# Input lines of the later parts turned by VectorE in square blocks, and the images loaded in another order of partitions

## The chip, the core and the metric

The kernel runs on one core of a Trainium2 chip. The metric is the device time of one execution in microseconds (us). Most of the work is fp32 matmuls on TensorE (PE); VectorE (DVE), ScalarE (ACT) and GpSimd (POOL) prepare operands and take results away, and SyncE (SP), POOL and ACT issue DMAs.

## What is computed

The input `x` holds 1024 images of 16 x 16 pixels with 16 channels, fp32. Four layers follow, each of them residual on a group-normalised input:

```
x = x + tt_matvec(gn(x), core0, core1, core2)   # layer 0, a tensor-train matrix
x = x + nca(gn(x), weights of L1)               # layer 1
x = x + conv3x3(gn(x), filters, bias)           # layer 2
x = x + nca(gn(x), weights of L3)               # layer 3
```

`gn` is a group norm with 8 groups of 2 channels over an image. The change is in how `x` gets into the kernel for layer 0, before and during that layer's first phase.

## The kernel before, in words

**Layout.** The batch is cut into two chunks of 512 images (`NB` = 512). In memory an image is one row of 4096 values, and a load puts one image on each partition. The matmuls want the transpose: a line `[128, 512]`, whose 128 partitions are 8 columns x 16 channels of one image row `h` and whose 512 elements are the images. A chunk has 32 lines, `(h, wh)` with `h` from 0 to 15 and `wh` 0 or 1 (left or right half of the row).

**Parts.** Layer 0 works on four parts of the lines. Part 0 is `wh = 0` with `h % 8 < 4`: 8 lines a chunk, kept on chip in the tile that `part_tile(0)` gives. All 32 lines are also written to the scratch tensors `xr[n]` in DRAM, from where the later parts and the residual of layer 0 are read back (`load_part`, line 937, from 75% of phase 1 on; `residual`, line 1063, in phases 2 and 3).

**`input_steps` (line 812)** gives the steps for a chunk:

- `load` (line 820): 8 DMAs of 1024 KB, each with 128 images by 8 image rows into one of 8 slots of `XN[1]`. Chunk 0 is loaded by SP, chunk 1 by POOL. A slot of chunk 1 overwrites the one of chunk 0, so a load waits until all readers of the slot are done.
- `stats` (line 827): 8 `bn_stats` on DVE for each slot.
- `turn(h, wh)` (line 836): four 128x128 transposes on PE (line 840) into one PSUM bank, and one copy by ACT into the on-chip part (line 843) or a `lines` tile (line 851). Two lines share one `lines` tile of tag `t4`, of which there are three (`gn = dict(t4=3, ...)`, line 1514), and leave by one POOL DMA of 512 KB (line 853); the on-chip lines leave four at a time by a POOL DMA of 1024 KB (line 845).
- `small`, `newton`, `widen`, `spread` (lines 857 to 890): mean and scale of each image and group, transposed to lines on PE and kept in `mr`.

`normed` (line 903) and `combined` (line 915) then normalise and add up part 0 on DVE.

**Order of the work.** Every engine works off its instructions in the order in which the program issues them. At the start (line 1541) the steps of chunk 0 up to `normed` and `combined` are issued at once (`now`), with 14 of the 32 turns of chunk 0. Then `run` (line 1479) issues phase 0 of layer 0: 64 main steps, four for each of 16 units (u0 to u15; a unit is one output tile pair). A main step is two `T.matmul` calls (four PE records, line 1098) of `pieces` (line 1082). In its first step a unit also builds the weights of the next one (`build`, line 1009: matmuls `pw` at line 1021, ACT copies at line 1026); in its third it asks SP for `gq` data two units ahead (`gload`); in its fourth DVE makes the mixed weight of the next unit (`mix`, line 1031, record L1039), and the next unit's first matmul reads that mixed weight. Between main steps `run` puts background steps, each with a cost: a step becomes due at the share of the main steps that equals the share of the costs ahead of it. In phase 0 the background is, in this order: what is left of chunk 0's turns (`late`) with the loads of chunk 1 among them, eight steps `later` that make the second half of the `g` weights (each pair uses a tile of tag `t4` that ACT fills, line 565), stats and turns of chunk 1 (`woven_in`), the small steps, and `normed` and `combined` for chunk 1. Phase 1 needs these last ones.

Of the kernel before, what the change touches and what calls it, by code (L numbers as in the profile page):

```python
# [19 lines left out]
P = 128  # L20
NB = 512
# [82 lines left out]
def conv_preact_kernel(ctx: ExitStack, tc: tile.TileContext, a: dict, out: bass.AP):  # L104
    nc = tc.nc
    V, A, G, T = nc.vector, nc.scalar, nc.gpsimd, nc.tensor
# [16 lines left out]
    xr = [dram.tile([2, S, P, NB], F32, tag=f"xr{n}", name=f"xr{n}") for n in range(NCH)]  # L123
# [12 lines left out]
    def work(shape, tag, name, dt=F32):  # L136
        p, sizes = pool["sb"]
        return p.tile(shape, dt, tag=tag, name=name, bufs=sizes[tag])
# [23 lines left out]
    ident = const.tile([P, P], F32, tag="ident", name="ident")  # L162
# [649 lines left out]
    def input_steps(n, tag, lag, queue):  # L812

        st = {}
        slots = XN[1].rearrange("p n b -> p (n b)").rearrange("p (s f) -> p s f", s=8)
        X, E = part_tile(0)

        def load(half, bg):  # L820
            b0 = n * NB + bg * P
            queue.dma_start(
                slots[:, 4 * half + bg],
                a["x"][b0 : b0 + P, 8 * half : 8 * half + 8].rearrange("b h w c -> b (h w c)"),
            )

        def stats(half, bg):
            if half == 0 and bg == 0:
                st["b"] = work([P, NB], "s", "bn")[:, 0:384].rearrange(
                    "p (g k f e) -> p g k f e", g=4, k=8, f=2  # L830
                )
            x = slots[:, 4 * half + bg].rearrange("p (q g i) -> p q g i", g=8, i=2)
            for g in range(8):
                V.bn_stats(st["b"][:, bg, g, half], x[:, :, g])

        def turn(h, wh):
            pt = bank([P, 4, P], tag[0], "ptin")
            for bg in range(4):
                x = slots[:, 4 * (h // 8) + bg].rearrange("p (h w f) -> p h w f", h=8, w=2)
                T.transpose(pt[:, bg], x[:, h % 8, wh], ident)  # L840
            pt = pt.rearrange("p g b -> p (g b)")
            if wh == 0 and h % 8 < 4:
                A.copy(X[:, h // 8, h % 4, 1], pt)
                if h % 4 == 3:
                    G.dma_start(
                        xr[n][0, h - 3 : h + 1].rearrange("h p b -> p h b"), X[:, h // 8, :, 1]
                    )
                return
            if h % 2 == 0:
                st["l"] = work([P, 2, NB], "t4", "lines")  # L850
            A.copy(st["l"][:, h % 2], pt)
            if h % 2 == 1:
                G.dma_start(
                    xr[n][wh, h - 1 : h + 1].rearrange("h p b -> p h b"), st["l"]
                )

        def small():
            t = work([P, NB], "n", "small")
            st["mv"] = t[:, 0:64].rearrange("p (g k e) -> p g k e", g=4, k=8)
            st["ve"], st["t"], st["r"] = (  # L860
                t[:, 64 + 32 * j : 96 + 32 * j].rearrange("p (g k) -> p g k", g=4) for j in range(3)
            )
            for bg in range(4):
                for g in range(8):
                    V.bn_aggr(st["mv"][:, bg, g], st["b"][:, bg, g])
            V.tensor_scalar(st["ve"], st["mv"][:, :, :, 1], GN_EPS, None, ALU.add)
            A.activation(st["t"], st["ve"], AF.Sqrt)

        def newton():
            ve, t, r = st["ve"], st["t"], st["r"]  # L870
            V.reciprocal(r, t)
            V.tensor_tensor(t, r, r, ALU.mult)
            V.tensor_tensor(t, t, ve, ALU.mult)
            V.tensor_scalar(t, t, -0.5, 1.5, ALU.mult, ALU.add)
            V.tensor_tensor(r, r, t, ALU.mult)

        def widen(k):
            st["e", k] = e = work([P, NB], "s", "wide").rearrange("p (g f) -> p g f", g=4)
            src = st["mv"][:, :, :, 0] if k == 0 else st["r"]
            for bg in range(4):  # L880
                V.tensor_copy(
                    e[:, bg].rearrange("p (w g i) -> p w g i", w=8, i=2),
                    src[:, bg].unsqueeze(1).unsqueeze(3).broadcast_to([P, 8, 8, 2]),
                )

        def spread(k):
            pt = bank([P, 4, P], tag[0], "ptmr")
            for bg in range(4):
                T.transpose(pt[:, bg], st["e", k][:, bg], ident)
            A.copy(mr[:, k, n], pt.rearrange("p g b -> p (g b)"))  # L890

        loads = [lambda half=half, bg=bg: load(half, bg) for half in range(2) for bg in range(4)]
        stat = [[(2.6, lambda half=half, bg=bg: stats(half, bg)) for bg in range(4)] for half in range(2)]

        lines = [
            [(1, lambda h=h, wh=wh: turn(h, wh)) for wh in range(2) for h in range(8 * half, 8 * half + 8)]
            for half in range(2)
        ]
        tail = [(3, small), 2, (1, newton), (1, lambda: widen(0)), (1, lambda: widen(1)), 1]
        tail += [(0, lambda: spread(0)), lag, (0, lambda: spread(1)), 2]  # L900
        return loads, stat, lines, tail

    def normed(p, n, src=None):

        X, E = part_tile(p)

        def op(b, t, k):
            x = X[:, b, t : t + 2, n]
            y = x if k or src is None else X[:, b, t : t + 2, src]
            m = mr[:, k, n].unsqueeze(1).broadcast_to([P, 2, NB])  # L910
            V.tensor_tensor(x, y, m, ALU.mult if k else ALU.subtract)  # L911

        return [(1.2, lambda b=b, t=t, k=k: op(b, t, k)) for b in range(2) for t in (0, 2) for k in range(2)]
# [605 lines left out]
    def now(steps):  # L1519
        for step in steps:  # L1520
            step = step[1] if isinstance(step, tuple) else step
            if callable(step):
                step()
# [8 lines left out]
    with ExitStack() as es:  # L1532
        stage(es, dict(gn, w=2, r=2, gq=2, R=1), dict(o=3, w=4, m=1))
        setup, later = train_setup(XN[0].rearrange("p n b -> p (n b)")[:, 8192:14336])
# [3 lines left out]

        A.activation(work([P, NB], "n", "warm")[:, 0:1], ident[:, 0:1], AF.Sqrt)
        now(setup[:1])  # L1540
        now(stat[0] + stat[1] + lines[0][:4] + setup[1:] + tail[:1] + lines[1][:4] + tail[1:] + lines[0][4:10])
        start, phases = layer_train()
        start()
        now(normed(0, 0, 1) + combined(0, True))
        tag[0] = "mw"
        late = lines[0][10:] + lines[1][4:]
        loads, stat, lines, tail = input_steps(1, tag, 2, G)
        woven_in = [x for j in range(2) for i in range(4) for x in stat[j][i : i + 1] + lines[j][4 * i : 4 * i + 4]]
        run(
            steps_of(phases[0]), 130, (),  # L1550
            (late[:6] + loads[0:4] + late[6:] + loads[4:] + later + woven_in + tail + normed(0, 1) + combined(0, False), 0.0, 1.0),
        )
        run(
            steps_of(phases[1]), 350, (),
# [82 lines left out]
```

## Time and profile before

| what | value |
|---|---|
| three runs, lowest, median, highest | 3052.58, 3054.53, 3059.36 us |
| the profiled execution's own time | 3054.15 us |
| its span | 3052.4 us (1.75 us lie around it) |
| busy PE, DVE, ACT, POOL | 2982.6, 1757.4, 1100.0, 674.8 us |
| PE first matmul of phase 0 | 50.13 us |
| PE in 50 to 218 us | phase 0 |

Times are us from the span's start unless said otherwise. A row of groups has, after the first bar, the busy us and the mean ns of one instruction, and after the second the idle time of its engine ahead of it and what ended that. In a timeline each row begins with its start and its length in us. Rows of DMA issues have the count, the KB of each and the median us to landing; rows of DMA queues have packets, MB and the share of 16 engines' time.

Where phase 0 ends can be read from two things. DVE's record L1039 comes once for each unit of phase 0; the four together at 216.19 us are for the first unit of phase 1, and are issued in the last unit of phase 0. And PE's `pw` of the second unit of phase 1 begins at 220.34 us, four PE records of about 0.43 us after phase 1 began, so that phase 0 ends at 218.6 us.

### The profile page before, as it was taken

To read this page: it belongs to the slowest core of one execution; us is meant where nothing else is said; L and a number is where in the kernel's file an instruction comes from. 1 tells how busy PE (TensorE), PEld (TensorE's weight loads), DVE (VectorE), ACT (ScalarE), POOL (GpSimd) and SP (SyncE) were. 2 spreads that over 40 slices of the span, in tenths; PEclk is the share of its full clock that TensorE was granted. 3 is DMA by queue.
4 is the path that set the end of the run, shared out by engine and by line. 5 is a ranking of instruction groups with operands and counts; after the bars stand their busy time and mean duration, and the time that the engine had idled before them with its cause. 6 is when DMAs were issued, how large, how long until landed. Compare 5 with 4: busy or idle time off the path is not lost.

```text
span 3052.4 us, 36639 instructions
## 1 busy us (share of the span) xinstructions
PE 2982.6 (98%) x13746; PEld 1252.2 (41%) x13746; DVE 1757.4 (58%) x2338; ACT 1100.0 (36%) x1798; POOL 674.8 (22%) x732
## 2 busy tenths in 40 slices
PE   7999999999999999999999999999999999999996
PEld 5544334444444444444444433333333333333332
DVE  5254336555554555544555768756977766856432
ACT  4431341100000000000111156666667656666563
POOL 1114671200000000000000015434542223442331
PEclk8999999999999999999999999999999999999998
DMA  7642664533333433332222235436337866343555
GB/s 260 257 146 88 137 140 156 179 107 116 109 110 126 151 109 109 109 102 88 88 88 94 71 123 172 132 123 202 123 125 177 193 101 204 123 129 112 149 163 197
DMA packets 251809, 418.67 MB, mean 137 GB/s; under 512 B 35044, under 2 KB 105320, under 8 KB 248560
## 3 DMA queue, kind: packets, MB, share of 16 engines
q1 hardware_dynamic: 225376, 362.45, 35.9%
q0 software_dynamic: 25440, 53.58, 8.5%
q8 instruction: 109, 1.79, 0.2%
q14 instruction: 68, 0.56, 0.1%
q10 hardware_dynamic: 816, 0.30, 0.0%
HBM read 238.79 MB, written 165.60 MB: 132 GB/s over the span
## 4 chain that ended last, share of the span: by engine, by line
issue 47%; PE 43%; POOL 5%; DMA 1%; DVE 1%; ACT 0%; SPq 0%; POOLq 0%; DVEq 0%
PE ph L1466 17%; PE po L1098 13%; PE po L1317 6%; PE po L1193 2%; POOL u L1368 2%; POOL res L1369 2%; PE pw L1021 1%; PE L_conv_pe L392 1%; PE ptin L840 1%; POOL xf L1242 1%; PE ptx L1378 1%; DMA gq<-g_dram 0%; PE pr L739 0%; PE pvar L727 0%; PE pmean L723 0%
## 5 line engine op out<-in xcount | busy, mean ns | idle before, releaser
L1098 PE MATMUL po<-xn,w 128*128 128x512 f32 x3584 | 1577.4, 597 | 4.6 <-DVE xn L911 4.6
L1098 PEld LDWEIGHTS po<-xn,w 128*128 128x128 f32 x3584 | 672.3, 191 | 841.5 <-issue 818.3
L1469 ACT ACTIVATE hid<-ph,pack 128x512 f32<-128x512 f32 x1024 | 652.5, 686 | 380.5 <-PE ph L1466 271.0
L1134 DVE TENSOR_TENSOR r<-r,po 128x512 f32<-128x512 f32 x576 | 378.1, 684 | 577.0 <-PE po L1098 525.9
L1368 POOL TENSOR_TENSOR u<-u,mask 128x512 f32<-128x512 f32 x124 | 195.8, 1579 | 1817.4 <-DMA nx<-xn 1239.7
L1026 ACT COPY w<-pw 128x512 f32<-128x512 f32 (+1 forms) x320 | 150.6, 557 | 1214.4 <-issue 1014.5
L1466 PE MATMUL ph<-xn,wq 32*128 32x512 f32 x3664 | 565.7, 610 | 0.0
L1466 PEld LDWEIGHTS ph<-xn,wq 32*128 32x128 f32 x3664 | 232.8, 184 | 270.2 <-issue 238.2
L1466 PE MATMUL ph<-xn,pack 32*128 32x512 f32 x1288 | 297.5, 623 | 1.2 <-DVE mask L1362 0.9
L1317 PE MATMUL po<-hid,pack 128*32 128x512 f32 x2048 | 282.5, 606 | 2.7 <-ACT hid L1469 2.7
L1039 DVE TENSOR_TENSOR w<-w 128x512 f32<-128x512 f32 x320 | 210.5, 685 | 99.8 <-ACT w L1026 99.8
L640 DVE TENSOR_TENSOR xn<-xn,m 128x1024 f32<-128x1024 f32 x160 | 225.5, 1458 | 47.1 <-ACT m L655 47.0
L1329 DVE SCALAR_TENSOR_TENSOR u<-po,pack,xn 128x512 f32<-128x512 f32 x128 | 95.9, 749 | 204.7 <-PE po L1317 200.3
L1369 POOL TENSOR_TENSOR res<-res,u 128x512 f32<-128x512 f32 x124 | 207.5, 1673 | 9.7
L1193 PE MATMUL po<-xn,convw 128*128 128x512 f32 x368 | 166.8, 606 | 5.1 <-ACT conv L1241 5.1
L1466 PEld LDWEIGHTS ph<-xn,pack 32*128 32x128 f32 x1288 | 115.8, 185 | 98.4 <-issue 62.7
L1134 DVE TENSOR_TENSOR xn<-xn,po 128x512 f32<-128x512 f32 x96 | 64.4, 685 | 125.9 <-PE po L1098 125.8
L1317 PEld LDWEIGHTS po<-hid,pack 128*32 128x32 f32 x2048 | 43.1, 109 | 197.4 <-issue 137.7
L607 DVE TENSOR_TENSOR sq<-sq 128x1024 f32<-128x1024 f32 x78 | 106.9, 1370 | 13.1 <-ACT sq L625 10.8
L1193 PEld LDWEIGHTS po<-xn,convw 128*128 128x128 f32 x368 | 69.2, 193 | 102.1 <-issue 92.0
L404 POOL DMA_DIRECT2D L_conv_wy<-xn x160 | 88.8, 563 | 28.5 <-ACT xn L398 17.6
L1021 PE MATMUL pw<-R,gq 32*128 32x256 f32 (+1 forms) x1280 | 88.9, 383 | 2.3 <-DMA gq<-g_dram 2.3
(165 smaller groups left out, 1775.2 us busy)
## 6 DMA issues: line engine op xcount, KB each, us to landing
xf<-r SPq DMA_DIRECT2D x112, 512.0 KB, 3.9
xn<-xf SPq DMA_DIRECT2D x96, 512.0 KB, 5.0
r<-xf SPq DMA_DIRECT2D x80, 512.0 KB, 4.4
wq<-L_conv_wy SPq DMA_DIRECT2D x192, 192.0 KB, 2.7
res<-xf SPq DMA_DIRECT2D x128, 256.0 KB, 3.0
xf<-res SPq DMA_DIRECT2D x96, 256.0 KB, 2.0
res<-xr SPq DMA_DIRECT2D x256, 64.0 KB, 2.8
xf<-conv POOLq DMA_DIRECT2D x64, 256.0 KB, 6.0
```

The lines of the kernel that those rows point to most:

```text
L640: V.tensor_tensor(part, part, m().unsqueeze(1).broadcast_to([P, 2, NB]), op)
L1021: T.matmul(pw[r][:, v], st["g", u][rows, v], st["R"][rows, p % 2, 64 * k0 : 256], start=True, stop=True,)
L1026: A.copy(w[:, k0:4, :, 32 * r : 32 * r + 32].rearrange("p k t (v o) -> p v (k t) o", v=2), pw[r],)
L1039: V.tensor_tensor(w[:, k], w[:, x], w[:, y], ALU.add if sign > 0 else ALU.subtract)
L1098: T.matmul(po, st["w", u][:, matrix, t], x, start=t == 0, stop=t == 3)
L1134: V.tensor_tensor(r[at], r[at], po, ALU.add if sign > 0 else ALU.subtract)
L1193: T.matmul(st["po", h][wh], conv["fw"][:, y], X[:, 16 * wh + h + y - 1], start=y == max(0, 1 - h), stop=y == min(2, S - h),)
L1317: T.matmul(po[32 * j : 32 * j + 32], nca["w1"][:, v], hid[j], start=v == 0, stop=v == 1)
L1368: by.tensor_tensor(u, u, st["m"][:, w2], ALU.mult)
L1369: by.tensor_tensor(r, r, u, ALU.add)
L1466: T.matmul(ph, w, x, start=k == 0, stop=k == len(tiles) - 1)
L1469: A.activation(h, ph, AF.Relu, bias=nca["bt"][:, r : r + 1])
```

## The change

Only eight lines a chunk are still turned on PE: the lines of part 0 that stay on chip. The other 24 are turned by DVE in 32x32 blocks, written into a `t4` tile and sent to `xr` by POOL. A block transpose moves values only inside a group of 32 partitions, so the images are loaded in another order: partition `32g + j` of slot `bg` holds image `128g + 32bg + j` of the chunk. With that, a block row of 32 partitions gives 128 successive images of a line. The lines turned on PE and the means and scales come out in the order of partitions, and ACT's copy puts them into the order of images (`ordered`, `in_order`).

In numbers, for each chunk:

- loads: 32 DMAs of 256 KB in place of 8 of 1024 KB
- turns on PE: 8 in place of 32
- `blocks(h)`, new: 16 steps. For `h % 8 < 4` only the right half (4 transposes of 128x128 elements, 4 DMAs), else both halves (4 transposes of 128x256 elements, 8 DMAs); each takes one whole `t4` tile. A DMA carries 64 KB: 32 partitions, 4 columns, 128 images.
- stores by POOL: 98 in place of 14

In the start, six turns of chunk 0 disappear, and the order in phase 0 is put together again: 16 `blocks` steps of chunk 0 at a cost of 2.2 each with the loads of chunk 1 among them, then `later`, then stats, 8 turns and 16 `blocks` of chunk 1.

```diff
         def load(half, bg):
-            b0 = n * NB + bg * P
-            queue.dma_start(
-                slots[:, 4 * half + bg],
-                a["x"][b0 : b0 + P, 8 * half : 8 * half + 8].rearrange("b h w c -> b (h w c)"),
-            )
+            for g in range(4):
+                b0 = n * NB + P * g + 32 * bg
+                queue.dma_start(
+                    slots[32 * g : 32 * g + 32, 4 * half + bg],
+                    a["x"][b0 : b0 + 32, 8 * half : 8 * half + 8].rearrange("b h w c -> b (h w c)"),
+                )
...
+        def in_order(pt):
+            return pt.rearrange("p s (g j) -> p g s j", g=4)
+
+        def ordered(x):
+            return x.rearrange("p (g s j) -> p g s j", g=4, s=4)
+
-        def turn(h, wh):
+        def turn(h):
             pt = bank([P, 4, P], tag[0], "ptin")
             for bg in range(4):
                 x = slots[:, 4 * (h // 8) + bg].rearrange("p (h w f) -> p h w f", h=8, w=2)
-                T.transpose(pt[:, bg], x[:, h % 8, wh], ident)
-            pt = pt.rearrange("p g b -> p (g b)")
-            if wh == 0 and h % 8 < 4:
-                A.copy(X[:, h // 8, h % 4, 1], pt)
-                if h % 4 == 3:
+                T.transpose(pt[:, bg], x[:, h % 8, 0], ident)
+            A.copy(ordered(X[:, h // 8, h % 4, 1]), in_order(pt))
+            if h % 4 == 3:
+                G.dma_start(
+                    xr[n][0, h - 3 : h + 1].rearrange("h p b -> p h b"), X[:, h // 8, :, 1]
+                )
+
+        def blocks(h):
+            w0 = 4 if h % 8 < 4 else 0
+            t = work([P, 2, NB], "t4", "lines").rearrange("p a (w s j) -> p (a w) s j", s=4, j=32)
+            for bg in range(4):
+                x = slots[:, 4 * (h // 8) + bg].rearrange("p (h w f) -> p h w f", h=8, f=32)
+                V.transpose(t[:, w0:8, bg], x[:, h % 8, w0:8])
+            for wh in range(w0 // 4, 2):
+                for g in range(4):
                     G.dma_start(
-                        xr[n][0, h - 3 : h + 1].rearrange("h p b -> p h b"), X[:, h // 8, :, 1]
+                        xr[n][wh, h].rearrange("(w f) b -> f w b", f=32)[:, :, P * g : P * g + P],
+                        t[32 * g : 32 * g + 32, 4 * wh : 4 * wh + 4].rearrange("p w s j -> p w (s j)"),
                     )
-                return
-            if h % 2 == 0:
-                st["l"] = work([P, 2, NB], "t4", "lines")
-            A.copy(st["l"][:, h % 2], pt)
-            if h % 2 == 1:
-                G.dma_start(
-                    xr[n][wh, h - 1 : h + 1].rearrange("h p b -> p h b"), st["l"]
-                )
...
-            A.copy(mr[:, k, n], pt.rearrange("p g b -> p (g b)"))
+            A.copy(ordered(mr[:, k, n]), in_order(pt))
...
         lines = [
-            [(1, lambda h=h, wh=wh: turn(h, wh)) for wh in range(2) for h in range(8 * half, 8 * half + 8)]
+            [(1, lambda h=h: turn(h)) for h in range(8 * half, 8 * half + 4)]
+            + [(2.2, lambda h=h: blocks(h)) for h in range(8 * half, 8 * half + 8)]
             for half in range(2)
         ]
...
-        now(stat[0] + stat[1] + lines[0][:4] + setup[1:] + tail[:1] + lines[1][:4] + tail[1:] + lines[0][4:10])
+        now(stat[0] + stat[1] + lines[0][:4] + setup[1:] + tail[:1] + lines[1][:4] + tail[1:])
...
-        late = lines[0][10:] + lines[1][4:]
+        late = lines[0][4:] + lines[1][4:]
...
-        woven_in = [x for j in range(2) for i in range(4) for x in stat[j][i : i + 1] + lines[j][4 * i : 4 * i + 4]]
+        woven_in = [x for j in range(2) for i in range(4) for x in stat[j][i : i + 1] + lines[j][3 * i : 3 * i + 3]]
...
-            (late[:6] + loads[0:4] + late[6:] + loads[4:] + later + woven_in + tail + normed(0, 1) + combined(0, False), 0.0, 1.0),
+            (late[:8] + loads[0:4] + late[8:] + loads[4:] + later + woven_in + tail + normed(0, 1) + combined(0, False), 0.0, 1.0),
```

## The prediction

> **What bounds the kernel now.** I read the page's busy shares first, then the chain of waits in the first 240 us, where all that changes lies, then rows of groups and the timeline.
>
> ```profile
> PE 2982.6 (98%) x13746; PEld 1252.2 (41%) x13746; DVE 1757.4 (58%) x2338; ACT 1100.0 (36%) x1798; POOL 674.8 (22%) x732
> ```
> ```profile
> by line: PE po L1098 51.4%; PE ptin L840 9.5%; DMA gq<-g_dram 5.2%; PE pw L1021 5.0%; issue 3.7%; PE pg L561 3.3%; ACT w L1026 1.0%; SPq L1004 0.5%; PE ptmr L889 0.4%; PE L_conv_pt L287 0.3%; ACT r L1123 0.2%; SPq L1077 0.1%
> ```
> PE sets the pace, and its turns (L840) are on the chain with 9.5% of 240 us, 23 us. Their price and what could hold the new way up, from the groups of the first 420 us:
>
> ```profile
> L840 PE MATMUL ptin<-ident,xn 128*128 128x128 f32 x256 | 38.8, 300 | 1.8 <-ACT w L1026 1.8
> L853 POOL DMA_DIRECT2D xr<-lines x24 | 17.2, 716 | 90.1 <-ACT lines L851 88.2 <-ACT small L867 1.8
> L404 POOL DMA_DIRECT2D L_conv_wy<-xn x103 | 57.2, 564 | 7.7 <-DMA L_conv_wy<-xn 2.8 <-issue 2.4 <-ACT xn L398 1.3
> ```
> The reader is to see that POOL issues few large stores and mostly waits (88.2 us for ACT), and that a small POOL DMA of 48 KB (L404) still costs 564 ns of issue, against 716 for 512 KB. DVE's timeline has one mixed weight for each unit, which gives the length of a unit:
>
> ```profile
> 131.12 0.69 DVE L1039 TENSOR_TENSOR w<-w 128x512 f32<-128x512 f32 x1 [6.63 <-ACT w L1026]
> 141.06 0.69 DVE L1039 TENSOR_TENSOR w<-w 128x512 f32<-128x512 f32 x1 [6.63 <-ACT w L1026]
> ...
> 201.12 0.69 DVE L1039 TENSOR_TENSOR w<-w 128x512 f32<-128x512 f32 x1
> 208.78 0.69 DVE L1039 TENSOR_TENSOR w<-w 128x512 f32<-128x512 f32 x1
> ```
> The first unit has four turns beside it and lasts 9.94 us, the second none and lasts 7.66 us. A turn costs (9.94 - 7.66) / 4 = **0.57 us** of PE.
>
> [...] L404 lands after 2.5 us. [...] the 512-byte runs of L404 take about 100 us of one DMA engine a MB, chunk 1's loads and 2-KB stores (60 to 100 us) 425 / 9.82 = 43. [...] PE has little work from 78 to 81 us, and until about 87 us the granted clock is 0.5.
>
> **The change part by part.**
>
> *Turns taken from PE.* 32 - 8 = 24 fewer a chunk, 48 in all: 6 at the start, 42 in phase 0 (50 before, 8 after). At the start they lie between `spread` and the first `pw` (40.25 to 43.97 us), on the path to the first matmul at 50.13: it comes 4.0 us earlier, at 46.1. In phase 0: 42 x 0.57 = 24 us. So **28 us** is the ceiling. ACT loses 48 copies at 0.59 us; it isn't the bound.
>
> *Transposes added to DVE.* The nearest row:
>
> ```profile
> L969 DVE STREAM_TRANSPOSE xo<-xs x64: 632/658/747, 2781.9 to 3014.7; 128x256 f32<-128x256 f32 x64
> ```
> A full `blocks` step is 4 x 0.66 = 2.6 us, a half one about 1.4; a chunk 8 x 4.0 = 32 us, both 64. L969 reads with a stride, the new one doesn't, so it may be half as long; I take the row. DVE idles over half of phase 0, so the work alone hides. If that cover is gone, it adds at most the 1 to 3 us of a block ahead of a mixed weight.
>
> *Stores on POOL.* 4 x 8 + 8 x 8 = 96 a chunk. Price: L404's 0.56 us (also many 512-byte runs); bounds 0.49 (32-partition issue, L542) and 0.72 (L853). With chunk 1's loads, 32 x 0.5 (L542) = 16 us, POOL gets 192 x 0.56 + 16 = **124 us** of issue, against 24 x 0.72 + 8 x 0.57 = 22 before. That would fit into 168 us of phase 0, but the order of steps bunches it: the 16 blocks of chunk 0 are 35.2 of 140.4 of the background's cost, so with the loads they fall due in u0 to u4. DMAs to issue, by `run`'s arithmetic: u0 24, u1 28, u2 24, u3 36, u4 16. A unit of 7.66 us has room for 14.
>
> *The wait that comes with it.* `blocks` k needs the `t4` tile of `blocks` k-3, free when its last store has landed. DVE works in order, so a mixed weight issued after it waits too, and behind it PE's next unit. Worked out (POOL 0.56, landing 2.5 after issue):
>
> - DVE ends chunk 0's `combined` at 59.5 - 4 = 55.5; the first block is ready at 57. POOL is then never idle: 48 stores of the first eight blocks to 84, 16 loads to 92, then stores of h8, h9, h10 to 94, 96, 98.5.
> - h3 waits for h0's stores: the weight for u1 is there at 64 (PE ready at about 58). h7 waits for h4: u2 at 77. u3 at 85.
> - h8's stores are behind 4 MB of loads (10 us at the 420 GB/s of the trace), land at 97; h11, h12 follow, h13 waits for h10 until 101.4; the weight for u4 comes at **104.7**. Without waits PE would begin u4 at 57.6 + 3 x 7.66 = 80.6. So **24 us of the 28 are lost** by here.
> - u4 on: 12 units x 7.66 = 91.9; `later`'s matmuls 64 records x 0.128 (16 in 2.05 us) = 8.2; 8 turns 4.6; two `spread` 1.0; half clock after the wait of 12 us, 3.2 (as at 81 to 87 us before); ACT's `later` copies wait for `t4` tiles behind h13 to h15's stores, 3. Sum 111.9, to 216.6. Chunk 1's stores begin near 140 and POOL is free enough then; DVE gets to `small` without holding PE.
> - The landings are slower where DMA is full (before, `xr` stores 3.8 and `gq` 9.1 us median at 60 to 100 us): for h8 and h13 I add 2 us. Phase 0 ends at **218.6**, as before[...].
>
> *Loads of chunk 0 in quarters.* SP issues 32 instead of 8; its 32-partition DMAs (`gq`) go out at 0.54 us each, 17 us against 15.2 now, and the loads land until 31 us, so issue hides. If 32-partition loads ran worse, all of the start shifts: bounds -2 to +4, taken 0. *ACT's copies in image order* keep runs of 32; taken at 0 (16 + 4 copies, under 0.1 us each, under cover of PE). *Later stages*: same `xr`, same tiles; 0. POOL is done with stores by about 190 us, and its next waits for DVE ended at 220.
>
> Sum: 0 to +1 us on the profiled 3054.15 (which stands 0.4 below the median): **3055 us**; own range 3047 to 3063, for POOL's issue at 0.50 to 0.62 over the 68 DMAs that u4 waits for (-4 to +4) and the extra terms of 8 us.
>
> **The rivals.**
>
> *Slower: the DMA engines, not POOL's issue, pace u0 to u3.* Full-rate L404 shows its price:
>
> ```profile
> DMA packets 1709, 2.85 MB, mean 142 GB/s; under 512 B 681, under 2 KB 711, under 8 KB 1708
> ...
> q0 software_dynamic: 999, 1.55, 51.1%
> ```
> In that stretch of 20 us 0.511 x 320 = 164 us of engine time went into 37 or fewer DMAs of 48 KB, 4.4 us each or more, so 5.9 to 6.8 for 64 KB: 0.37 to 0.42 us of all 16. From 57 to 105 us: 80 stores 34, loads 10, three units of `m_dram` stores 4, `gq` 4: 52 us in 48. If it is over 1, landings stretch and POOL's own pace no longer counts; a store at 0.55 us of 16 engines makes 62, +14 us: **3068**. It decides from about 0.40 on. For: in the windows DMA was already 0.8 busy there. Against: L404's landings stay at 2.5 us at POOL's full rate.
>
> *Part of the gain stays.* POOL at 0.50 (-4), no half clock (-3), no wait of ACT (-3): **3045**. For: rows at 0.49. Against: L404's minimum is 562 ns.
>
> *The change does what it says.* DVE is never held long, PE gains all 28: **3026**. For: DVE and POOL are idle most of phase 0. Against: 36 DMAs in u3.
>
> *A slower start.* Quarter loads keep the last `stats` from ending: +8, **3063**.
>
> **How the numbers follow.** Forecast 0.42, slower rival 0.25, part 0.18, all 0.10, start 0.05. Within 0.2% (6 us, about what a measurement of this kernel can tell from no change): 0.30, all from the forecast's case; faster 0.05 of it, and 0.18 and 0.10, is 0.33; slower 0.07 of it, 0.25 and 0.05, is 0.37. Cases of both signs hold most of it; the likeliest's own range is above. Of the whole, 3041 to 3074 leaves out the full gain (0.10) and the tails of the slower and the partial case (0.10).
>
> **What would show it.** First `po` at about 46; POOL issuing without a gap from 57 to about 92 us and 96 stores by 119; DVE waiting for `xr<-lines` DMAs, PE for DVE L1039, the longest before u4 (about 12 us, at 93 to 105); PE clock at half after it; phase 0 ending at 217 to 220. Wrong: no such waits of PE (then towards 3026), or stores landing after 5 us or more, with DMA share at 1 (then 3068).

## The result and the profile after

The changed kernel takes **3095.81 us** (median of 4 runs, 3091.9 to 3096.03), the kernel before beside it 3056.66: ratio **1.0126**, 95% interval 1.0109 to 1.0144. It is slower, and 22 us above the upper end of the predicted range. The profiled execution took 3096.03 us, with a span of 3094.3 against 3052.4: 41.9 us more to account for. Executions of one and the same kernel differ by some us with the clock that TensorE is granted: of 93 of the kernel before, all in the fast state, the shortest (3050.3 us) shows a mean of 0.989 and the longest (3063.82 us) 0.985, and a trace shows one execution only.

From the page of the kernel after, the busy shares, the clock, the chain and two groups:

```profile
PE 2978.4 (96%) x13554; PEld 1236.0 (40%) x13554; DVE 1793.7 (58%) x2466; ACT 1076.0 (35%) x1750; POOL 773.9 (25%) x924
...
PEclk6799999999999999999999999999999999999998
...
issue 47%; PE 40%; POOL 6%; DMA 2%; DVE 2%; SPq 0%; ACT 0%; POOLq 0%; DVEq 0%
...
L1113 PE MATMUL po<-xn,w 128*128 128x512 f32 x3584 | 1584.8, 600 | 36.4 <-DVE w L1054 31.4
...
L866 POOL DMA_DIRECT2D xr<-lines x192 | 104.0, 550 | 27.1 <-DVE lines L863 18.0
```
PE has 192 instructions fewer and is hardly less busy (98% before), so work was taken from it and waiting put in its place: 31.4 us ahead of `po` for the mixed weight. The granted clock is 0.6 and 0.7 in the first two slices, where it was 0.8 and 0.9. The 192 stores are there at 550 ns each.

**The start.** Statistics of chunk 0, whose last instruction begins when the last load is in (times of the first and last start at the end of the line), before and after; then the same 12 us before and after (last columns: clock, DMA share, GB/s):

```profile
L834 DVE BATCH_NORM_STATS2 bn<-xn x64: 401/408/427, 6.4 to 33.5; 128x6 f32<-128x256 f32 x64
```
```profile
L836 DVE BATCH_NORM_STATS2 bn<-xn x64: 405/409/428, 12.3 to 50.7; 128x6 f32<-128x256 f32 x64
```
```profile
20.00:32.00 12.00, 12.00 (x79) 11.41 (x78) 9.73 (x30) 6.53 (x12) 3.77 (x7) 0.73 1.01 391
```
```profile
20.00:32.00 12.00, 4.67 (x20) 4.10 (x21) 6.23 (x19) 2.35 (x4) 0.28 (x1) 0.50 1.02 218
```
The statistics end 17.2 us later. The DMA engines are busy all the time, as before (1.01), but move 218 GB/s where they moved 391. GB/s counts all transfers of the stretch; before, that includes stores of `g` and of lines. While its loads ran alone (16 to 20 us), they moved 426.

**Phase 0.** PE's timeline after, the four pieces that waited longest or began a stage:

```profile
63.41 3.78 PE L1113 MATMUL po<-xn,w 128*128 128x512 f32 x4 [4.04 <-DVE xn L926]
79.21 3.18 PE L1113 MATMUL po<-xn,w 128*128 128x512 f32 x4 [3.79 <-DVE w L1054]
...
130.10 3.78 PE L1113 MATMUL po<-xn,w 128*128 128x512 f32 x4 [23.54 <-DVE w L1054]
169.80 1.82 PE L1036 MATMUL pw<-R,gq 32*128 32x128 f32 x16 [6.97 <-DMA gq<-g_dram]
```
The first `po` is at 63.41 instead of 50.13 (+13.3), and the unit u4 waits 23.54 us for a weight. DVE's timeline at that place, and POOL's:

```profile
103.67 0.89 DVE L863 STREAM_TRANSPOSE lines<-xn 128x128 f32<-128x128 f32 x4 [5.15 <-DMA xr<-lines]
124.70 0.89 DVE L863 STREAM_TRANSPOSE lines<-xn 128x128 f32<-128x128 f32 x4 [20.13 <-DMA xr<-lines]
```
```profile
73.91 25.96 POOL L866 DMA_DIRECT2D xr<-lines  x48 [16.91 <-DVE lines L863]
99.86 3.42 POOL L824 DMA_DIRECT2D xn<-in_x_dram  x7
...
110.75 0.49 POOL L824 DMA_DIRECT2D xn<-in_x_dram  x1 [1.18 <-issue]
...
115.25 0.57 POOL L866 DMA_DIRECT2D xr<-lines  x1 [0.84 <-DMA xn<-in_x_dram]
...
120.50 0.55 POOL L866 DMA_DIRECT2D xr<-lines  x1 [1.37 <-DMA xn<-in_x_dram]
```
POOL issues 48 stores without a gap, seven loads of chunk 1, and from then on only one DMA in about 1.2 us, in step with loads that land. The stores of block h8 stand behind all 16 loads, and DVE's next four transposes wait 20.13 us for them; the mixed weight for u4 follows those and eight more on DVE and begins at 129.40. With the wait, phase 0 ends at 255.2 (the second `pw` of phase 1 at 256.94, less 1.72 as for the kernel before) against 218.6: it lasts 191.8 us instead of 168.5. So the 41.9 us are **13.3 at the start, 23.3 in phase 0** and 5.3 later. Of those 5.3, 3.3 arise while the kernel before goes from 327.2 to 463.9 us: both kernels do the same 505 PE records there, PE is without work for 1 us in both, and the granted clock is 1.00 before and 0.98 after. Why it is lower isn't shown.

### The profile page after: what moved, and what is told of

It is laid out like the page before. It is cut to its first block, busy times and chain, and to the rows that moved or that the text cites. A ratio compares the mean times of both kernels' runs of the same rounds, so it can differ in the third digit from the quotient of the medians.

```text
span 3094.3 us, 36704 instructions
## 1 busy us (share of the span) xinstructions
PE 2978.4 (96%) x13554; PEld 1236.0 (40%) x13554; DVE 1793.7 (58%) x2466; ACT 1076.0 (35%) x1750; POOL 773.9 (25%) x924
## 4 chain that ended last, share of the span: by engine, by line
issue 47%; PE 40%; POOL 6%; DMA 2%; DVE 2%; SPq 0%; ACT 0%; POOLq 0%; DVEq 0%
PE ph L1481 17%; PE po L1113 11%; PE po L1332 6%; POOL res L1384 2%; POOL u L1383 2%; PE po L1208 2%; POOL xr L866 1%; DMA xn<-in_x_dram 1%; PE L_conv_pe L392 1%; POOL xf L1257 1%; PE pw L1036 1%; PE ptx L1393 1%; DVE xn L926 1%; DMA xn<-xf 0%; PE pr L739 0%
## 5 line engine op out<-in xcount | busy, mean ns | idle before, releaser
L1113 PE MATMUL po<-xn,w 128*128 128x512 f32 x3584 | 1584.8, 600 | 36.4 <-DVE w L1054 31.4
L866 POOL DMA_DIRECT2D xr<-lines x192 | 104.0, 550 | 27.1 <-DVE lines L863 18.0
L404 POOL DMA_DIRECT2D L_conv_wy<-xn x160 | 88.8, 563 | 30.1 <-ACT xn L398 17.5
```

Of the source, the lines that this page charges most:

```text
L866: G.dma_start(xr[n][wh, h].rearrange("(w f) b -> f w b", f=32)[:, :, P * g : P * g + P], t[32 * g : 32 * g + 32, 4 * wh : 4 * wh + 4].rear ...
L1113: T.matmul(po, st["w", u][:, matrix, t], x, start=t == 0, stop=t == 3)
```

## The experiments

All runs beside the kernel before on the same chip; the chips differ, so versions are compared by their ratios or by their distance from the kernel before beside them. GB/s is of all transfers from 20 to 32 us; phase 0's end is read as above; "before" and "after" name the kernel from which a version starts.

| run | what differs | ratio (95%) | GB/s | first `po` | phase 0 ends |
|---|---|---|---|---|---|
| before | | 1 | 391 | 50.13 | 218.6 |
| after | | 1.0126 (1.0109–1.0144) | 218 | 63.41 | 255.2 |
| quarters | before + quarter loads | 1.0088 (1.0073–1.0103) | 221 | 67.61 | 245.6 |
| strided | quarters, every 4th image and partition | 1.0074 (1.0059–1.0089) | 393 | 74.02 | 239.3 |
| halves | before + loads of 64 partitions | 1.0086 (1.0070–1.0102) | 224 | 66.12 | 241.0 |
| rows of 2 KB | before + 32 loads of 128 partitions | 1.0030 (1.0017–1.0044) | 391 | 55.47 | 224.0 |
| opposite | quarters, SP 0–63, ACT 64–127 | 1.0083 (1.0068–1.0098) | 233 | 69.46 | 249.1 |
| same half | quarters, SP 0–31 and 64–95, ACT the others | 1.0096 (1.0082–1.0111) | 234 | 73.10 | 252.3 |
| far places | quarters into every 4th partition | 1.0072 (1.0056–1.0088) | 392 | 72.75 | 240.2 |
| far images | quarters of every 4th image | 1.0094 (1.0076–1.0112) | 215 | 69.87 | 248.1 |
| whole | after + whole loads | 1.0032 (1.0020–1.0043) | 397 | 46.12 | 231.3 |
| merged | whole + 4 stores a block | 1.0031 (1.0020–1.0043) | 394 | 45.48 | 230.5 |
| one store | whole + 1 store a block, 2-KB runs | 0.9965 (0.9954–0.9976) | 373 | 45.48 | 206.0 |
| spread | merged + loads between blocks | 0.9997 (0.9988–1.0007) | 371 | 45.37 | 216.3 |
| two queues | spread + half the stores on SP | 1.0039 (1.0024–1.0055) | 385 | 46.15 | 237.8 |
| long rows | one store, lines read in block order | 1.0059 (1.0044–1.0073) | 380 | 45.34 | 215.8 |
| swapped | long rows, short transfers on the other queues | 1.0016 (1.0009–1.0024) | 379 | 45.54 | 226.1 |

Where phase 0's length goes, as an estimate from the windows of 1 us of each trace: of PE's busy time, the share that the granted clock left out (one less the clock) is time lost to the clock, the rest is work at full clock; what isn't busy is without work.

| run | phase 0, us | work at full clock | without work | lost to the clock |
|---|---|---|---|---|
| before | 168.5 | 156.3 | 4.5 | 7.7 |
| after | 191.8 | 138.8 | 39.8 | 13.2 |
| quarters | 178.0 | 156.8 | 11.5 | 9.6 |
| whole | 185.2 | 138.2 | 30.6 | 16.3 |
| one store | 160.5 | 139.8 | 12.2 | 8.6 |
| spread | 170.9 | 138.9 | 22.5 | 9.5 |
| two queues | 191.7 | 141.3 | 22.6 | 27.7 |

### Which half of the change costs: the loads alone, and the change without them

Quarters in the kernel before, images left where they are:

```
-            b0 = n * NB + bg * P
-            queue.dma_start(
-                slots[:, 4 * half + bg],
-                a["x"][b0 : b0 + P, 8 * half : 8 * half + 8].rearrange("b h w c -> b (h w c)"),
-            )
+            for g in range(4):
+                b0 = n * NB + bg * P + 32 * g
+                queue.dma_start(
+                    slots[32 * g : 32 * g + 32, 4 * half + bg],
+                    a["x"][b0 : b0 + 32, 8 * half : 8 * half + 8].rearrange("b h w c -> b (h w c)"),
+                )
```


> The kernel before, with only its loads cut into quarters of 32 successive partitions (256 KB each), images and everything else as they were. Theory (such quarter loads run at half the rate, about 215 GB/s against 420): the last load ends near 48 us instead of 31, phase 0 begins near 67, and chunk 1's loads hold DMA longer; 3072 to 3082 us. Rival (the lost time is POOL's issue and the 512-byte stores, and the late start has another cause): start as before, 3052 to 3060.

3085.24 us: the loads alone make the kernel before 27 us slower, 17.5 of them by the first `po` and 9.5 in phase 0, where chunk 1 is loaded the same way: PE waits there once 4.4 us for ACT's copy into a `lines` tile, and 4.9 us in all for `gq` (2.3 before).

The other way round, the change with whole loads. Partition p of slot s then holds image 4p + s, the transposes write with a stride of four, the stores stay:

```
-                queue.dma_start(
-                    slots[32 * g : 32 * g + 32, 4 * half + bg],
...
+            src = a["x"][n * NB : n * NB + NB, 8 * half : 8 * half + 8]
+            queue.dma_start(
+                slots[:, 4 * half + bg], src.rearrange("(p s) h w c -> s p (h w c)", s=4)[bg]
+            )
...
-                V.transpose(t[:, w0:8, bg], x[:, h % 8, w0:8])
+                V.transpose(t[:, w0:8, :, bg], x[:, h % 8, w0:8])
```


> The changed kernel with whole loads of 128 partitions: slot s holds on partition p image 4p + s of the chunk, and the transposes write with a step of four elements so that the stores are the same. Theory of the loads: phase 0 begins at 46 to 47 us, the wait ahead of the fifth unit falls from 23 us to 12 or less, and the time is what the prediction had without the slow loads, 3050 to 3062. Rival (POOL's issue and 512-byte stores make the loss in phase 0): only the start comes back, 3074 to 3082.

3067.62 us: 28 of the change's 39 us are gone, and about 10 over the kernel before remain. In the traces, 17.3 of them go at the first `po` and 6.6 in phase 0; the rest lies later. PE's timeline of this run:

```profile
46.12 3.78 PE L1111 MATMUL po<-xn,w 128*128 128x512 f32 x4 [4.04 <-DVE xn L924]
...
62.59 3.78 PE L1111 MATMUL po<-xn,w 128*128 128x512 f32 x4 [4.45 <-DVE w L1052]
74.36 1.98 PE L1111 MATMUL po<-xn,w 128*128 128x512 f32 x4 [1.14 <-DVE w L1052]
107.51 3.78 PE L1111 MATMUL po<-xn,w 128*128 128x512 f32 x4 [17.40 <-DVE w L1052]
```
This is nearly the course that the prediction worked out: the same places, with the wait ahead of u4 longer (17.40 against some 12) and the one ahead of u2 shorter. The rest is taken up under the stores.

### Why the loads are slow

My first explanations were that a DMA of few rows is slow, or that each DMA has a fixed cost. Four kernels, all the kernel before with another shape of load: quarters that take every fourth image to every fourth partition (`slots[g:P:4]` from `x[b0 + g : b0 + P : 4]`), halves of 64 successive partitions, and 32 loads of 256 KB that each reach all 128 partitions with rows of 2 KB instead of 8.

> The kernel before, with its loads cut into four of 256 KB each, but each takes every fourth partition, so that it spreads over all 128; images as before. If it is the block of 32 successive partitions that is slow: loads end near 31 us, 3052 to 3060. If any load of 32 rows is slow for its size: as with the quarters of successive partitions, 3072 to 3082.

> The kernel before with its loads cut into halves of 64 partitions (512 KB). If a load costs a fixed time on the DMA engines beside its bytes, the two runs known (8 loads end at 31 us, 32 at 48) put that at (48.2 - 31.2) / 24 = 0.7 us, and 16 loads end near 37: phase 0 about 6 us later, 3060 to 3068. If only loads of 32 rows are slow, the end stays at 31 to 32: 3053 to 3058.

> The kernel before with 32 loads a chunk of 256 KB as in the quarters, but each over all 128 partitions, with two image rows (2 KB) of each image. If the cost is fixed for each load: loads end near 48 us, 3075 to 3087, as with the quarters. If it comes from the few rows that each DMA engine gets of a 32-row load[...]: loads end near 31 to 36, 3053 to 3065.

The same 12 us of each, in the order strided, halves, rows of 2 KB:

```profile
20.00:32.00 12.00, 9.83 (x44) 9.27 (x45) 0.00 (x0) 4.11 (x7) 3.77 (x7) 0.50 0.99 393
```
```profile
20.00:32.00 12.00, 7.56 (x34) 6.29 (x33) 6.10 (x19) 4.28 (x9) 1.40 (x2) 0.72 1.02 224
```
```profile
20.00:32.00 12.00, 12.00 (x75) 11.47 (x72) 8.13 (x24) 6.18 (x12) 3.77 (x7) 0.68 1.04 391
```
Both explanations fall with the strided run: the same 32 DMAs of 256 KB, with 32 rows each, run at 393 GB/s (401 from 16 to 28 us, when nothing but SP's queue moves), so neither their size nor their number nor the few rows set the rate. And halves of 512 KB run no faster than quarters. Time alone would have misled in the strided run: there all statistics waited for the last load (DVE is at 0.00 above, and begins at 36.0 us), so it is as slow as the quarters at nearly twice their rate.

The run with rows of 2 KB says less than its 391 suggests, as a store of lines by POOL runs beside its loads from 22 us on. The kernel before and this run, while SP's loads were nearly alone:

```profile
16.00:20.00 4.00, 4.00 (x27) 3.04 (x25) 1.74 (x6) 3.50 (x9) 0.00 (x0) 1.00 1.01 426
```
```profile
12.00:20.00 8.00, 5.31 (x32) 3.44 (x31) 5.37 (x16) 6.52 (x14) 0.00 (x0) 1.00 0.88 260
```
So these loads are slow too, with the DMA engines 0.88 busy, and the first `po` comes 5 us later than before. What holds them isn't shown.

The strided run changed the images read as well as the partitions written. Two kernels change one each. Far places, against the quarters:

```
-                    slots[32 * g : 32 * g + 32, 4 * half + bg],
+                    slots[g : P : 4, 4 * half + bg],
```
Far images, against the quarters:

```
-                b0 = n * NB + bg * P + 32 * g
+                b0 = n * NB + bg * P
...
-                    a["x"][b0 : b0 + 32, 8 * half : 8 * half + 8].rearrange("b h w c -> b (h w c)"),
+                    a["x"][b0 + g : b0 + P : 4, 8 * half : 8 * half + 8].rearrange("b h w c -> b (h w c)"),
```


> The run with quarters of 32 successive images (3085 us), each quarter written to every fourth partition instead of 32 successive ones, the images read being the same 32 successive ones; the images so stand in a wrong order, nothing else changes. If the partitions reached set the rate: about 390 to 410 GB/s, as in the run where images and partitions were both strided. If the rows read in HBM set it (32 successive images, 512 KB in a row, instead of images spread over 2 MB): still 215 to 225 GB/s, last statistics beginning near 48 us.

> The other half of the cross: every fourth image of a block of 128 is read, as in the strided run, and written to 32 successive partitions; the images so stand in a wrong order, nothing else changes. If the partitions reached set the rate: 215 to 225 GB/s, last statistics beginning near 48 us, 3081 to 3088 us. If the rows read in HBM set it: 390 to 410 GB/s.

Far places, then far images:

```profile
20.00:32.00 12.00, 9.55 (x44) 9.25 (x45) 0.00 (x0) 4.11 (x7) 3.78 (x7) 0.53 1.00 392
```
```profile
20.00:32.00 12.00, 2.88 (x12) 2.48 (x13) 7.56 (x23) 1.17 (x2) 0.00 (x0) 0.58 1.01 215
```
The partitions written decide between the two rates; the rows read do not. In numbers: 215 to 224 GB/s for 32 and for 64 successive partitions, and 400 to 426 where rows of 8 KB go to partitions from all of 0 to 127 and the loads are alone. Why 64 successive ones are no faster than 32 isn't shown.

If a transfer is held by the partitions that it reaches, two transfers to opposite halves might go side by side. I expected that, and that two in the same half stay at the rate of one, the first case of the second expectation. The edit to the quarters (for the same half, `g % 2` stands in place of `g >= 2`):

```
+                q = nc.scalar if n == 0 and g >= 2 else queue
-                queue.dma_start(
+                q.dma_start(
```


> The kernel before with loads of chunk 0 in quarters of 32 successive partitions; quarters 0 and 1 (partitions 0 to 63) are issued by SP, quarters 2 and 3 (64 to 127) by ACT, so that at any time one load of each half of the partitions is in flight. Chunk 1's quarters all on POOL, as in the run with quarters alone (3085 us). Theory that a load's rate is set by the partitions it reaches[...]: the two queues together read at about 400 GB/s, the last statistics begin at 31 to 34 us instead of 48, and some 14 to 17 us of the loss come back: 3066 to 3072 us. Rival (32 rows at a time keep each queue's packets slow, or HBM reads in this order are slow): 215 to 225 GB/s, 3083 to 3087 us.

> As the run with opposite halves, but SP issues quarters 0 and 2 and ACT quarters 1 and 3: two queues as there, the same 16 loads each, but at any time both loads are in the same half of the partitions (as long as the queues keep step). [...] still 215 to 230 GB/s, last statistics begin at 46 to 49 us, 3081 to 3087 us. Rival (two queues are faster than one whatever the partitions): about 400 GB/s as with opposite halves, and the same time as that run, 3066 to 3072 us.

Opposite halves, then the run called same half:

```profile
20.00:32.00 12.00, 0.00 (x0) 0.00 (x0) 7.35 (x24) 0.00 (x0) 0.00 (x0) 1.00 1.02 233
```
```profile
20.00:32.00 12.00, 0.00 (x0) 0.00 (x0) 7.96 (x24) 0.00 (x0) 0.00 (x0) 0.50 1.03 234
```
My expectation fell: 233 against 234 GB/s, 5% over one queue (221). What holds two queues together at this rate isn't shown. The same-half run is no clean case of one half. In the run with opposite halves a load took about 9 us to land (medians of 8.8 on SP's queue and 9.2 on ACT's from 20 to 28 us), and each queue issued four in those 8 us; as an estimate from that, each queue of the same-half run had loads of both halves pending. The other run is enough: with one half on each queue, SP's moved 0.98 MB from 20 to 28 us and ACT's 0.90, side by side, and the rate stays at 233. Their first `po` isn't earlier than in the run with quarters, and can't be compared closely: ACT issues loads until 38 us, and its copies come after.

### Where the rest goes: the stores

With whole loads the change still takes about 10 us more than the kernel before, where the prediction had 28 less as the ceiling. Merging the two halves of a full block's stores (128 KB each, 128 stores instead of 192) takes POOL issue away. One store for each block in runs of 2 KB takes away the short runs and most of the number too; that kernel writes the values to wrong places of the lines.

Merged, against whole (`xq` is `xr` with the two halves of a line side by side):

```
-            for wh in range(w0 // 4, 2):
-                for g in range(4):
...
+            for g in range(4):
+                G.dma_start(
+                    xq[n][h, w0 // 4 : 2].rearrange("a (w f) b -> f (a w) b", f=32)[:, :, P * g : P * g + P],
+                    t[32 * g : 32 * g + 32, w0:8].rearrange("p w j s -> p w (j s)"),
+                )
```
One store, against whole:

```
-            for wh in range(w0 // 4, 2):
-                for g in range(4):
...
+            wh = w0 // 4
+            G.dma_start(
+                xr[n][wh:2, h].rearrange("a p b -> p a b"),
+                t[:, w0:8].rearrange("p (a w) j s -> p a (w j s)", w=4),
+            )
```


> The same with whole loads, and a full block step leaves by 4 stores of 128 KB instead of 8 of 64 KB (still 512-byte runs; the scratch tensor has its two halves of a row side by side). If POOL's issue holds what is left of phase 0: POOL has 64 stores a chunk at 0.65 us instead of 96 at 0.55, and 10 to 20 us come off the run with whole loads. If the DMA engines' work on 512-byte runs holds it: within 4 us of that run.

> The changed kernel with whole loads, where each block step leaves by one DMA of up to 512 KB in runs of 2 KB over all partitions; it leaves out the right arrangement of the lines (values land at wrong places of the same lines), so only its time counts. If what is left of the loss is the number of stores and their 512-byte runs: no wait of PE ahead of the fifth unit, 3030 to 3045. If it is DVE's own transposes, or the order of steps (second loads beside the g weights): 3055 to 3066.

Merged: 3066.89 us, the same as with 192 stores. The number is that of the second expectation, but not for its reason: with fewer stores to issue (568 ns each, where 650 was expected) PE reached the long wait's end 6 us earlier, and lost that again, as its timeline shows, by waiting for `later`'s copies, whose `g` tiles share the ring of `t4` with the blocks:

```profile
101.54 3.78 PE L1111 MATMUL po<-xn,w 128*128 128x512 f32 x4 [12.82 <-DVE w L1052]
124.43 1.22 PE L1034 MATMUL pw<-R,gq 32*128 32x128 f32 x10 [5.47 <-ACT g L566]
```
One store: 3044.06 us, and phase 0 ends at 206.0. Beside the kernel before, whole is 9.4 us over and this run 11.9 us under, so the form of the stores costs some 21 us. How much of it is the run length and how much the number isn't separated; the step from 192 to 128 alone brought nothing. The transposes are all there, so this run also shows what the change is worth with long stores: 11 to 12 us less than the kernel before. PE is without work for 12.2 us of phase 0 here, against 30.6 with whole loads.

Can that be had? Three attempts in turn. First another order, `later` ahead of the blocks and chunk 1's loads one at a time between them; then half the stores on SP:

```
+        first = [x for i in range(4) for x in loads[i : i + 1] + late[8 + 2 * i : 10 + 2 * i]]
...
+            for x in loads[4 + i : 5 + i] * (j == 0) + stat[j][i : i + 1] + lines[j][3 * i : 3 * i + 3]
...
-            (late[:8] + loads[0:4] + late[8:] + loads[4:] + later + woven_in + tail + normed(0, 1) + combined(0, False), 0.0, 1.0),
+            (later + late[:8] + first + woven_in + tail + normed(0, 1) + combined(0, False), 0.0, 1.0),
```
```
-                G.dma_start(
+                (nc.sync if g >= 2 else G).dma_start(
```


> The kernel with whole loads and merged stores in another order: the g weights ahead of the blocks of chunk 0, and chunk 1's loads one at a time between the blocks instead of four in a row. If the loss that is left comes from four loads in a row holding POOL and from loads landing beside the g weights' stores: 3035 to 3050. If it comes from the amount of stores whatever their order: 3060 to 3068, as with merged stores.

> The version with whole 128-partition loads, four stores of 128 KB for a full block and chunk 1's loads spread between the blocks (3054.7 us), with two of the four stores of each block issued by SP instead of POOL. If POOL's issue time and its queue behind the loads hold the tiles (theory), the tiles come free earlier: the wait before u4 falls from 10 us to under 5, and the time to 3042 to 3051 us, faster than the kernel before. Rival: SP waits in order for DVE's transposes and the loads of gq queue behind it, so that PE waits for pw instead: 3057 to 3070 us.

Spread and two queues, waits of PE in phase 0 (total us, times, longest):

```profile
PE po L1111 <- DVE w L1052: 15.7, 6, 9.9
PE ptin L849 <- DMA xn<-in_x_dram: 6.3, 1, 6.3
```
```profile
PE pw L1034 <- DMA gq<-g_dram: 21.0, 12, 6.3
...
PE po L1111 <- DVE w L1052: 1.0, 2, 0.6
```
The order brings 10 us (3054.68; ratio 0.9997 against 1.0031), level with the kernel before. With SP's help the waits for weights are gone (15.7 to 1.0 us), but the rival came: SP waits in order for DVE, `gq` queues behind it, and PE waits 21 us for that (3070.97 us; the profiled execution is the slowest of six, 3077.5).

Last, the long runs with right values: the stores of the run with one store, the order of the run spread, and the lines left in block order in HBM, for the readers to put in order with short transfers. Of a part's loads and of part 0's stores:

```
+    def images(x):
+        return x.rearrange("p (g b) -> p g b", g=4)
...
+    def places(n, a, h, w):
+        return xr[n][a, h].rearrange("(g f) (w b) -> w f g b", f=32, b=P)[w]
...
+            G.dma_start(places(n, 0, h, w), images(X[32 * w : 32 * w + 32, h // 8, h % 4, 1]))
...
+            for i in range(4):
+                for w in range(4):
+                    nc.sync.dma_start(
+                        images(X[32 * w : 32 * w + 32, b, i, n]),
+                        places(n, p // 2, 8 * b + 4 * (p % 2) + i, w),
+                    )
```
Swapped is the same with the two queues exchanged, `nc.sync` for part 0's stores and `G` for the part loads.

> Whole loads, one store of 256 or 512 KB for each block in runs of 2 KB (as in the run at 3044 us, which wrote to wrong places), the order of the run with the loads spread between the blocks, and the lines kept in that block order in HBM, so that the values are right: the readers of the later phases pay, with 64 loads of 64 KB a part instead of 4 of 1 MB, two residual loads for one, and 64 stores of 64 KB for part 0. If the stores of 512 byte runs are what phase 0 loses (theory) and the readers lie hidden: 3038 to 3048 us, faster than the kernel before. Rival: the short loads come late to DVE, or the 64 extra stores hold POOL as before: 3052 to 3075 us.

> The run with block lines in long rows (3072 us) with the two sets of short transfers on the other queue each: the 64 loads of a later part on POOL, which does little after 500 us, instead of SP, and the 64 stores of part 0 on SP instead of POOL. In that run phase 0 ended 3 us before the kernel before's, and PE then waited 4 to 5 us three times for gq behind the part loads on SP. Theory (the loss after phase 0 is SP's order alone, and POOL's part-0 stores hold the blocks in phase 0): no wait for gq over 2 us after phase 0, phase 0 ends 5 to 12 us before the kernel before's, and 3040 to 3052 us in all. Rival (short loads slow the reading of gq and residuals wherever they are issued): waits of 3 to 5 us remain, 3058 to 3072 us.

Long rows: SP's queue at the first loss after phase 0, and PE at that place:

```profile
480.18 16.27 SPq L965 DMA_DIRECT2D xn<-xr  x32
496.50 1.84 SPq L1028 DMA_DIRECT2D gq<-g_dram  x4
```
```profile
498.56 3.37 PE L1045 MATMUL pw<-R,gq 32*128 32x256 f32 x16 [3.91 <-DMA gq<-g_dram]
639.12 3.54 PE L1045 MATMUL pw<-R,gq 32*128 32x256 f32 x16 [5.35 <-DMA gq<-g_dram]
```
The run takes 3072.11 us. In the profiled execution, the slowest of five (3081.32), phase 0 ends 3 us before the kernel before's, and some 30 us are lost after it, 12.8 of them in three waits for `gq`. `gq` goes out after 32 part loads that held SP for 16.3 us. Swapped, PE waits for no `gq` after phase 0 and only about 2 us are lost there, so the loss came from the queue on which the short transfers stood and not from the transfers as such. But part 0's stores now stand before `gq` on SP in phase 0:

```profile
PE pw L1045 <- DMA gq<-g_dram: 10.2, 8, 2.9
PE po L1124 <- DVE w L1063: 6.8, 3, 2.8
```
Phase 0 ends 7.5 us later than before, and the run takes 3062.55. The time is in the rival's range, by a mechanism that neither expectation named. No version with right values beat the kernel before; the 11 us of the run with one store were not had. A mix, part loads and part 0's stores both on POOL, wasn't tried: an estimate from the two runs is a phase 0 3 us shorter and 2 us lost later, no change.

## Why the prediction was wrong

**The step that failed: "Loads of chunk 0 in quarters"**, "bounds -2 to +4, taken 0". It counted SP's issue (17 us against 15.2) and let the loads land until 31 us, as whole ones do. Issue did not hide: SP's 32 issues were spread over 36.9 us, 14.0 of them spent waiting for earlier loads. The rate was 218 GB/s instead of 391, and the start came 17.3 us later than with whole loads (63.41 against 46.12). The same step was left out for chunk 1: the first 16 of its loads were costed at 0.5 us of issue each and "10 us at the 420 GB/s", and held POOL from 99.9 to about 124. That is the 23.54-us wait, against 12 predicted; with whole loads it is 17.40, as stores also go out singly behind four loads of 1 MB (87.6 to 100.7 us on POOL). In all, slow loads make 28 of the 39 us. The sentence "If 32-partition loads ran worse, all of the start shifts" named the mechanism and then bounded it at 4 us without a row to bound it with: no load of the kernel before with this shape was large enough to show a rate. The fourth rival, a slower start, was right in kind and had 8 us and a chance of 0.05.

**What held, in the run with whole loads.** The first `po`: 46.1 predicted, 46.12. The 6 turns less at the start were worth the 4.0 us. The weights for the units u1 to u4: 64, 77, 85 and 104.7 predicted; in that run's trace they end at 62.5, 74.3, 82.1 and 107.5. The price of a store: 0.56 predicted, 0.55. The second rival (DMA engines as the bound) was wrong there: while POOL issues stores without a gap, the stores land after 2.0 us and DMA is 0.58 busy in all. This stretch of that run shows it:

```profile
101.00:122.00 21.00, 14.49 (x65) 8.06 (x65) 12.79 (x30) 3.54 (x8) 21.00 (x40) 0.73 0.58 122
```
That is at most 0.58 x 0.54 = 0.31 us of all engines a store, against the 0.37 to 0.42 of the prediction.

**What was mis-sized.** *A turn.* The 0.57 us divided the difference of two units by four turns, but the unit with turns also has a wait of PE for ACT in it. PE's timeline of the kernel before in that unit:

```profile
130.32 1.09 PE L840 MATMUL ptin<-ident,xn 128*128 128x128 f32 x8 [0.44 <-ACT w L1026]
...
134.68 0.60 PE L840 MATMUL ptin<-ident,xn 128*128 128x128 f32 x4
135.12 1.88 PE L1098 MATMUL po<-xn,w 128*128 128x512 f32 x4
```
A turn delays PE by 0.44 us. For 42 turns that is 18 us instead of 24, as the work at full clock shows (156.3 us before, 138.2 to 139.8 with the change); the ceiling was nearer 22 than 28.

*The stretch from u4 to the end of phase 0.* 111.9 us were predicted, and the run with whole loads took 231.3 - 107.5 = 123.8. The estimate by windows gives 106.6 us of work (predicted 105.7), 6.2 without work (3), and 11.0 lost to the clock (3.2). So the clock is the term most in error. From 123 to 141 us PE works, with no wait over 0.43 us, at a granted clock of 0.63, half of `later`'s matmuls among its work; the kernel before did all of `later`'s, from 98 to 114 us, at 1.00:

```profile
123.00:141.00 18.00, 17.57 (x64) 9.95 (x63) 5.33 (x17) 5.11 (x11) 2.02 (x4) 0.63 0.98 364
```
```profile
98.00:114.00 16.00, 15.56 (x96) 10.34 (x95) 4.92 (x14) 6.94 (x14) 0.00 (x0) 1.00 0.96 383
```
The prediction knew a low clock only from a stretch in which PE had little to do (busy 0.88 of the 3 us from 78 to 81 in the kernel before, then a clock of 0.51 from 81 to 87); here it came without one, and why isn't shown. The run spread, with `later` first and the loads apart, lost 9.5 us to the clock in all of phase 0 instead of 16.3, and was without work for 22.5 instead of 30.6.

*Transposes* were taken at 0.66 us, those of the last layer, which read with a stride of four elements; with images in groups the full ones took 0.41 and with a stride of four 0.61, and nothing hung on it. ACT's copies of the turned lines took 591 ns (median of 16) in image order, against 593 before, so that 0 was right. Units without turns follow each other every 7.72 us in the run with one store (predicted 7.66).

**Later stages** were taken at 0. Of the 41.9 us, 5.3 lie there, most of them at a lower granted clock as told above; with whole loads 13.0 - 12.7 = 0.3 do.

## What to carry to other kernels

When a load is cut by partitions, count its rate anew: 32 or 64 successive partitions moved at 215 to 234 GB/s where all 128 moved at 420 to 426, and neither a larger DMA nor a second queue made up for it. A reordering that needs other images in other places was had here from the source's side of a whole load (partition p of slot s takes image 4p + s), at the price of a strided write elsewhere (612 ns for a transpose instead of 411). And work moved off a busy engine paid only where the short stores that it brings were not queued ahead of something that the busy engine waits for: PE was spared 18 us of turns and waited 23.54 us for one weight, and two attempts that took stores off POOL's queue moved the wait from the weights to `gq` (21.0 us in one, 10.2 in the other). And a stretch's GB/s is that of the loads only while nothing else moves.

## What the runs showed of the hardware

- Loads with rows of 8 KB into 32 or 64 successive partitions: 215 to 224 GB/s with DMA 1.0 busy; into every fourth partition, alone, 400 to 401, and into all 128, 420 to 426. The DMA share doesn't show the difference, only GB/s does. Loads of rows of 2 KB into all 128: 260, with DMA 0.88 busy.
- Two queues with such loads in flight: 233 to 234 GB/s, whether each queue issues to one half of the partitions (233) or to both (234).
- With loads waiting on POOL's queue, POOL's later DMAs go out one by one as loads land, about 1.2 us apart in the kernel after. What holds them isn't shown.
- The granted clock can fall while PE works without a wait over 0.43 us (0.63 from 123 to 141 us of the run with whole loads), and 3050.3 and 3063.82 us of the unchanged kernel went with 0.989 and 0.985.
- A DVE transpose of 128x256 fp32 took 411 ns on average with contiguous blocks and 612 with a write stride of four elements; of 128x128, 278 and 392.
